# A graph network on 64 graphs: weight preparation in fifteen separately placed steps in place of five, and a second tile for a transposed weight

## Chip, cores and metric

The kernel runs on one core of one Trainium2 chip. The metric is the device time of one execution in microseconds (us), as the median of several runs.

## What is computed

The input is 64 graphs with 256 nodes each, 256 features per node, and a 256x256 adjacency matrix of zeros and ones for each. Two layers are applied. Cut to what matters:

```python
# layer 0: attention with relation masks, 8 heads
q, k = x @ Wq + bq, x @ Wk + bk
attn = softmax(q @ k.T / sqrt(32))
for r in range(4):
    out += (attn * (adj == r)) @ (x @ Wv[r] + bv[r])
x = ln(x + out @ Wo + bo) * g1 + beta1
x = ln(x + gelu(x @ W1 + b1) @ W2 + b2) * g2 + beta2
# layer 1: two graph-attention steps, then a feed-forward
def gat(h, W, a):
    Wh = h @ W
    e = leaky_relu(Wh @ a[:256] + (Wh @ a[256:]).T, 0.2)
    return softmax(where(adj > 0, e, -9e15), axis=1) @ Wh
h = gat(gat(x, L1_W1, a1), L1_W2, a2)
h = ln(x + h) * g_ln1 + b_ln1
y = ln(h + relu(h @ w_ff1 + b_ff1) @ w_ff2 + b_ff2) * g_ln2 + b_ln2
```

All is float32. The feed-forward layers have 1024 hidden features.

## The kernel before

The 64 graphs pass through one after another, as a pipeline: while the second feed-forward of one graph runs, the first of a later graph and the attention of a still later one run too. A graph in the tables of this text counts from 0.

*Stages of a graph.* `load_front` (L185-193) loads the features (`xin`, L190, four DMAs) and the adjacency (`adi`, L192). VectorE transposes the features (`xT`, L529). TensorE makes queries and keys (L558, `qk_ps`), ScalarE copies them out (L567, L569). There are two halves of four heads; for each half TensorE makes four score tiles (L606, `s`), VectorE their row maxima (`nmax`, L611), ScalarE the exponentials (L619, `e`), VectorE the reciprocals (`rden`, L624), ScalarE the normalisation (L629). VectorE transposes 32x32 squares (`eT_sq`, L340), and the rest of the transposition goes through DRAM: a write (L345) and a read (L349) on SyncE's queue (SP). VectorE multiplies by the mask (`pm`, L638), TensorE multiplies with the values (`po`, L653). The values come from `v_ps` (L582) with the weights in seven combinations, as in Strassen's product with seven multiplications. Then follow the output projection (`wo_ps`, L673), a layer norm (L398, the tile `y`), the first feed-forward (`ffa`: up L455, copies L466, adds L472, gelu L478, sums for the seven products on GpSimd L440 and L492, down L503, adds L511), a layer norm, the two graph-attention steps (`ga`, `gb`: L683 to L749, among them `ga_z` at L702, which opens with the copy of a TensorE result on ScalarE), a layer norm, the second feed-forward (`ffb`, with relu) and the last layer norm.

*Buffers.* The score tiles have four PSUM banks with one buffer each, so the second half's scores wait for the first half's exponentials. All other products take one of three PSUM buffers (`mm_tile`).

*Weights and their preparation.* The weights are loaded once by 49 DMAs, all on SP (L864). Some are then prepared once, since biases and gains of the layer norms are folded into the weights that follow:

- `v_weights`: ten VectorE operations that make the value weights' combinations.
- `out_bias` (L289-294): a product on TensorE (`bo_ps`, L292) and an addition.
- `gat_weights` (L296-320): a transposition of the second graph weight (`gw2T`, L303, copy L304), a small product with the attention vectors (`gu`, L311, copy L313), a transposition of the first graph weight (`gw1T`, same lines), and two products (`gext`, L318, copy L320). Both transposes are copied to one tile, `gw[:, 1]`.
- `ffn_weights`, once for each feed-forward (L247-268): 32 matmuls of one column each for the bias (`ffa_b_ps`, `ffb_b_ps`, L253), its addition on VectorE (L255), two activations on ScalarE that apply the gain (L257), four VectorE operations for the up-weights' combinations (L261 to L264), an addition to the row bias (L266), and four VectorE operations for the down-weights' combinations (L275 to L278).

*What sets the order.* The order is written out by hand. A table, `PLACES`, gives each operation of a graph a place; graph g adds g times `PERIOD`. `LOAD_PLACES` gives each weight load a place, and the names `V_PLACE`, `OUT_PLACE`, `GAT_PLACE`, `FFA_PLACE` and `FFB_PLACE` give one to each of the five preparations. Everything is sorted by place and issued in this order, and each engine executes its part in the order of issue. A place is a number for sorting, not a time. A whole preparation is issued at one place, so its instructions stand together on every engine.

Of the kernel before, what the change touches and what calls it, by code (L numbers as in the profile page):

```python
# [9 lines left out]
F32 = mybir.dt.float32  # L10
# [5 lines left out]
ALU = mybir.AluOpType  # L16
AX = mybir.AxisListType

P = 128
# [8 lines left out]
PERIOD = 46.802000  # L28
# [40 lines left out]
    "lg4": 380.3574, "lb4": 381.5864, "store": 394.4577, "te": 551.6675,  # L69
}  # L70
LOAD_PLACES = [
    105.247, 106.338, 251.305, 142.756, 226.120, 202.518, 180.231, 135.528, 193.356, 105.689, 128.568, 205.544,
    225.287, 220.197, 228.322, 220.191, 135.518, 134.198, 236.500, 236.497, 267.691, 145.759, 148.475, 184.117,
    188.115, 118.463, 185.107, 185.099, 138.353, 159.388, 289.336, 256.975, 248.494, 253.344, 263.500, 246.882,
    179.276, 264.537, 240.121, 150.635, 216.481, 224.999, 149.895, 193.794, 257.889, 277.220, 276.101, 310.307,
    239.224,
]
V_PLACE, OUT_PLACE, FFA_PLACE, GAT_PLACE, FFB_PLACE, ODD_PLACE = 135.857, 138.353, 239.224, 193.799, 285.406, 240.000

# [11 lines left out]
def binary_graphs(  # L93
# [13 lines left out]
    nc = tc.nc  # L107
    B, N, D = x.shape
    R = 2
    FF = W1.shape[1]  # L110
    H = 8
    DH = D // H
    KD = D // P
# [3 lines left out]
    EX = D + 4  # L117
    assert (N, D, FF, DH, C, HQ) == (256, 256, 1024, 32, 2, 4)

    const = ctx.enter_context(tc.tile_pool(name="const", bufs=1))  # L120
# [10 lines left out]
    def mm_tile(shape, name, dt=F32):  # L131
        return ps_mm.tile(shape, dt, tag="mm", name=name)
# [5 lines left out]
    ident = const.tile([P, P], F32, name="ident")  # L138
# [14 lines left out]
    def weight(w, name, mixed=False):  # L153

        k, n = w.shape[0] // P, w.shape[1]
        t = const.tile([P, k, n], F32, name=name)
        if mixed:
            mixed_rows(t, w)
        else:
            loads.append((t, w.rearrange("(k p) n -> p k n", p=P)))  # L160
        return t
# [5 lines left out]
    def mixed_vec(v, name):  # L167

        t = const.tile([P, KD, 1], F32, name=name)
        for a in range(A):  # L170
            src = bass.AP(tensor=v.tensor, offset=v.offset + a * S, ap=[[1, S], [P, KD], [1, 1]])
            loads.append((t[a::A], src))
        return t

    def rowvec(v, n, name):
        t = const.tile([P, n], F32, name=name)
        loads.append((t, _row(v, n)))
        return t

    def colvec(v, n, name):  # L180
        t = const.tile([P, n // P], F32, name=name)
        loads.append((t, _col(v, n)))
        return t
# [37 lines left out]
    be1_r, bl1_r = shifts[:, 0], shifts[:, 1]  # L221
    loads.append((be1_r, _row(beta1, D)))
    w1, b1_c = weight(W1, "w1", mixed=True), colvec(b1, FF, "b1_c")
    g1_c, be1_c = mixed_vec(g1, "g1_c"), mixed_vec(beta1, "be1_c")
    w2, b2_r = weight(W2, "w2"), rowvec(b2, D, "b2_r")
    w2_t, f2_t = (const.tile([P, 3, KF // 2, P], F32, name=f"{n}_t") for n in ("w2", "f2"))
    up_t = {n: const.tile([P, 3, FF // 2], F32, name=f"{n}_u") for n in ('ffa', 'ffb')}
    g2_r, be2_r = rowvec(g2, D, "g2_r"), rowvec(beta2, D, "be2_r")
    gw = bp.tile([P, 2, KD, D], F32, tag="ff", name="gw", bufs=3)
    gw1 = gw[:, 0]  # L230
    mixed_rows(gw1, gW1)
    gx = bp.tile([P, KD, EX], F32, tag="wh", name="gx", bufs=2)
    loads.append((gx[:, :, :D], gW2.rearrange("(k p) n -> p k n", p=P)))
    a2c = const.tile([P, KD, 2], F32, name="a2c")
# [4 lines left out]
    gext = const.tile([P, KD, EX], F32, name="gext")  # L239
    gl1_r = rowvec(g_ln1, D, "gl1_r")  # L240
    loads.append((bl1_r, _row(b_ln1, D)))
    f1, bf1_c = weight(w_ff1, "f1", mixed=True), colvec(b_ff1, FF, "bf1_c")
    gl1_c, bl1_c = mixed_vec(g_ln1, "gl1_c"), mixed_vec(b_ln1, "bl1_c")
    f2, bf2_r = weight(w_ff2, "f2"), rowvec(b_ff2, D, "bf2_r")
    gl2_r, bl2_r = rowvec(g_ln2, D, "gl2_r"), rowvec(b_ln2, D, "bl2_r")

    def ffn_weights(w, b, gain, shift, row, shift_row, name, wb, wb_t):  # L247


        p = mm_tile([P, KF], f"{name}_b_ps")  # L250
        for f in range(KF):
            for k in range(KD):
                nc.tensor.matmul(p[:, f:f + 1], w[:, k, f * P:(f + 1) * P], shift[:, k],  # L253
                                 start=(k == 0), stop=(k == KD - 1))
        nc.vector.tensor_tensor(b, p, b, ALU.add)  # L255
        for k in range(KD):
            nc.scalar.activation(w[:, k], w[:, k], AF.Copy, scale=gain[:, k])  # L257
        if name in up_t:
            (a11, a21), (a12, a22) = ([w[:, k, i * FF // 2:(i + 1) * FF // 2] for i in range(2)] for k in range(KD))
            s1, s2, s4 = (up_t[name][:, i] for i in range(3))  # L260
            nc.vector.tensor_tensor(s1, a21, a22, ALU.add)  # L261
            nc.vector.tensor_tensor(s2, s1, a11, ALU.subtract)
            nc.vector.tensor_tensor(s4, a12, s2, ALU.subtract)
            nc.vector.tensor_tensor(a21, a11, a21, ALU.subtract)  # L264
            up_w[name] = {1: a11, 2: a12, 3: s4, 4: a22, 5: s1, 6: s2, 7: a21}
        nc.vector.tensor_tensor(row, row, shift_row, ALU.add)  # L266
        seven[name] = seven_weights([[wb[:, h * KF // 2:(h + 1) * KF // 2, d * P:(d + 1) * P] for d in range(2)]
                                     for h in range(2)], [wb_t[:, i] for i in range(3)])

    seven, up_w = {}, {}  # L270

    def seven_weights(b, t):


        nc.vector.tensor_tensor(t[0], b[0][1], b[1][1], ALU.add)  # L275
        nc.vector.tensor_tensor(t[1], t[0], b[0][0], ALU.subtract)
        nc.vector.tensor_tensor(t[2], b[1][0], t[1], ALU.subtract)
        nc.vector.tensor_tensor(b[0][1], b[0][0], b[0][1], ALU.subtract)  # L278
        return {1: b[0][0], 2: b[1][0], 3: t[2], 4: b[1][1], 5: t[0], 6: t[1], 7: b[0][1]}
# [13 lines left out]
                             start=(k == 0), stop=(k == KD - 1))  # L293
        nc.vector.tensor_tensor(bo_r, p, bo_r, ALU.add)

    def gat_weights():  # L296


        def transposed(w, t, name):
            pt = mm_tile([P, KD, D], f"{name}_ps")  # L300
            for k in range(KD):
                for f in range(KD):
                    nc.tensor.transpose(pt[:, f, k * P:(k + 1) * P], w[:, k, f * P:(f + 1) * P], ident)  # L303
            nc.vector.tensor_copy(t, pt)  # L304
            return t

        w2T = transposed(gx, gw[:, 1], "gw2T")
        pu = mm_tile([P, KD, 2], "gu_ps")
        for k in range(KD):
            for f in range(KD):  # L310
                nc.tensor.matmul(pu[:, k, :], w2T[:, f, k * P:(k + 1) * P], a2c[:, f, :],  # L311
                                 start=(f == 0), stop=(f == KD - 1))
        nc.vector.tensor_copy(gx[:, :, D:D + 2], pu)  # L313
        w1T = transposed(gw1, gw[:, 1], "gw1T")
        for k in range(KD):
            p = mm_tile([P, EX], f"gext_ps{k}")
            for f in range(KD):
                nc.tensor.matmul(p, w1T[:, f, k * P:(k + 1) * P], gx[:, f, :],  # L318
                                 start=(f == 0), stop=(f == KD - 1))
            nc.vector.tensor_copy(gext[:, k, :], p)  # L320

    class Transposed:  # L330

# [181 lines left out]
    class Graph:  # L513
# [166 lines left out]
        def gat_product(self, c):  # L680
            p = self.ps["ga", c] = mm_tile([P, EX], f"ga{self.g}_wps{c}")
            for k in range(KD):
                nc.tensor.matmul(p, self.ht.t[:, c, k, :], gext[:, k, :],  # L683
                                 start=(k == 0), stop=(k == KD - 1))
# [177 lines left out]

    assert len(loads) == len(LOAD_PLACES)
    plan = [(t, len(PLACES), lambda i=i: nc.sync.dma_start(*loads[i])) for i, t in enumerate(LOAD_PLACES)]  # L864
    for place, f in (
            (V_PLACE, v_weights),
            (OUT_PLACE, out_bias),
            ((B - 1) * PERIOD + ODD_PLACE, any_odd),
            (GAT_PLACE, gat_weights),
            (FFA_PLACE, lambda: ffn_weights(w1, b1_c, g1_c, be1_c, b2_r, be1_r, "ffa", w2, w2_t)),  # L870
            (FFB_PLACE, lambda: ffn_weights(f1, bf1_c, gl1_c, bl1_c, bf2_r, bl1_r, "ffb", f2, f2_t))):
        plan.append((place, len(PLACES), f))
    for g in range(B):
        ops = Graph(g).operations()
# [208 lines left out]
@with_exitstack  # L1083
def kernel(ctx: ExitStack, tc: tile.TileContext, *args):
    nc = tc.nc
    pool = ctx.enter_context(tc.tile_pool(name="odd", bufs=1))
    odd = pool.tile([P, 1], I32, name="odd")
    binary_graphs(tc, odd, *args)
    flag = nc.values_load(odd[0:1, 0:1], min_val=0, max_val=1)
    with tc.If(flag > 0):  # L1090
        any_graphs(tc, *args)
# [29 lines left out]
```

## Time and profile before

| what | value |
|---|---|
| median of 3 runs | 3115.67 us (3115.14 to 3116.3) |
| profiled execution | 3118.7 us, its span 3116.9 us |
| TensorE (PE) busy | 3020.8 us (97%), 24797 matmuls |
| VectorE (DVE) busy | 2618.7 us (84%) |
| ScalarE (ACT) busy | 2597.0 us (83%) |
| GpSimd (POOL) busy | 2364.2 us (76%) |
| mean granted TensorE clock | 0.987 |
| data moved by DMA | 457.16 MB, mean 147 GB/s |
| eT write, issue to landing | 3.1 us median |
| eT read, issue to landing | 3.6 us median |

The span is the time from the first to the last event of the profiled execution; 1.8 us of its 3118.7 lie outside it. Busy times are sums over the whole span. In a list of waits, the time is that in which an engine did nothing before the named instruction, and the name behind the arrow is what ended the idle time. The granted clock is the share of full speed at which TensorE was allowed to run; 0.50 is half clock.

### The profile page before, as it was taken

The numbers are of one execution on the slowest core, as the hardware profiler recorded it, in microseconds if no ns is written. First come the engines' busy times: TensorE is split into PE (matmuls) and PEld (weight loads), VectorE is DVE, ScalarE is ACT, GpSimd is POOL, SyncE is SP. The second block draws the span as 40 slices with busy tenths as digits, with TensorE's granted clock in tenths as the row PEclk, the third lists the DMA queues.
The fourth block names the chain that finished last, engine by engine and source line by source line (L and its number), as shares of the span: only waits on it lengthen the run. The fifth ranks groups of instructions, "written<-read, shape, count | busy, mean of one in ns | idle before, by whom it ended". The sixth has DMA issues, their size and how long they took to land.

```text
span 3116.9 us, 72178 instructions
## 1 busy us (share of the span) xinstructions
PE 3020.8 (97%) x24797; PEld 2611.0 (84%) x24797; DVE 2618.7 (84%) x5545; ACT 2597.0 (83%) x7109; POOL 2364.2 (76%) x3142
## 2 busy tenths in 40 slices
PE   6899999999999999999999999999999999999985
PEld 4688888888888888888888888888888888888874
DVE  6888888888888888888888888888888888888852
ACT  5688888888888888888888888888888888888852
POOL 1577777877877877877877877877878777787763
PEclk8899999999999999999999999999999999999997
DMA  7554555455455455455455455455455555445410
GB/s 188 163 158 144 145 162 151 144 160 152 142 157 161 136 160 161 137 157 155 135 160 156 140 156 154 142 154 158 145 147 159 146 146 162 147 143 162 143 50 27
DMA packets 808371, 457.16 MB, mean 147 GB/s; under 512 B 334529, under 2 KB 717377, under 8 KB 808001
## 3 DMA queue, kind: packets, MB, share of 16 engines
q1 hardware_dynamic: 808000, 452.49, 50.3%
q8 instruction: 200, 3.28, 0.5%
q14 instruction: 171, 1.39, 0.1%
HBM read 242.63 MB, written 201.33 MB: 142 GB/s over the span
## 4 chain that ended last, share of the span: by engine, by line
PE 93%; DMA 2%; DVE 2%; ACT 2%; POOL 1%; issue 1%; SPq 0%; POOLq 0%; DVEq 0%; ACTq 0%
PE ffb_ps L455 14%; PE ffa_ps L455 13%; PE ffb_po L503 7%; PE po L653 7%; PE qk_ps L558 7%; PE ffa_po L503 7%; PE v_ps L582 6%; PE ffa_pq L503 6%; PE ffb_pq L503 5%; PE s L606 4%; PE wo_ps L673 4%; PE h_ps L730 4%; PE h_ps L745 3%; PE ga_wps L683 3%; DMA ffa_T<-ffa_T_d 1%
## 5 line engine op out<-in xcount | busy, mean ns | idle before, releaser
L619 ACT ACTIVATE e<-s,nmax 128x256 f32<-128x256 f32 x1024 | 473.6, 476 | 10.6 <-DVE nmax L611 10.4
L629 ACT ACTIVATE e<-e,rden 128x256 f32<-128x256 f32 x1024 | 447.6, 502 | 25.0 <-DVE rden L624 25.0
L638 DVE TENSOR_TENSOR pm<-eT,adT 128x512 f32<-128x512 f32 x512 | 449.5, 899 | 0.0
L340 DVE STREAM_TRANSPOSE eT_sq<-e 128x512 f32<-128x512 f32 x512 | 349.1, 691 | 7.3 <-ACT e L629 6.0
L611 DVE TENSOR_REDUCE nmax<-s 128x2 f32<-128x512 f32 x512 | 341.7, 669 | 2.0 <-PE s L606 2.0
L478 ACT ACTIVATE ffb_h<-ffb_h,bf_c 128x256 f32<-128x256 f32 x512 | 224.9, 503 | 49.0 <-DVE ffb_h L472 49.0
L492 POOL TENSOR_TENSOR ffb_t<-ffb_h 128x512 f32<-128x512 f32 x64 | 81.5, 1273 | 225.8 <-ACT ffb_h L478 225.8
L466 ACT COPY ffb_h<-ffb_ps 128x512 f32<-128x512 f32 x256 | 151.0, 590 | 99.6 <-PE ffb_ps L455 99.5
L472 DVE TENSOR_TENSOR ffb_h<-ffb_ps,ffb_h 128x512 f32<-128x512 f32 x192 | 132.8, 692 | 107.2 <-PE ffb_ps L455 104.2
L466 ACT COPY ffa_h<-ffa_ps 128x512 f32<-128x512 f32 x256 | 148.3, 579 | 83.5 <-PE ffa_ps L455 47.8
L492 POOL TENSOR_TENSOR ffa_t<-ffa_h 128x512 f32<-128x512 f32 x64 | 82.5, 1289 | 172.6 <-PE ffb_pq L503 155.0
L619 ACT ACTIVATION_READ_ACCUMULATOR e<-s,nmax 128x1 f32 x1024 | 211.5, 207 | 0.0
L478 ACT ACTIVATE ffa_h<-ffa_h,b_c 128x256 f32<-128x256 f32 x512 | 211.1, 506 | 0.1
L472 DVE TENSOR_TENSOR ffa_h<-ffa_ps,ffa_h 128x512 f32<-128x512 f32 x192 | 132.3, 689 | 79.7 <-ACT ffa_h L466 45.8
L388 POOL TENSOR_TENSOR rs_x<-rs_x,nhalf 128x2 f32<-128x2 f32 x256 | 182.5, 713 | 21.3
L492 POOL TENSOR_TENSOR ffb_t<-ffb_h,ffb_t 128x512 f32<-128x512 f32 x128 | 163.6, 1278 | 36.3 <-ACT ffb_h L478 35.6
L492 POOL TENSOR_TENSOR ffa_t<-ffa_h,ffa_t 128x512 f32<-128x512 f32 x128 | 185.0, 1445 | 5.0
L591 DVE TENSOR_TENSOR v<-v,v_ps 128x256 f32<-128x256 f32 x448 | 177.2, 407 | 2.0 <-PE v_ps L582 1.1
L398 ACT ACTIVATE ffa_res<-ffa_res,nb_x,rs_x 128x256 f32<-128x256 f32 x256 | 139.9, 595 | 25.2 <-POOL nb_x L393 24.8
L455 PE MATMUL ffb_ps<-ffb_T,f 128*128 128x128 f32 x1024 | 130.7, 283 | 26.7 <-DMA ffb_T<-ffb_T_d 22.9
L606 PE MATMUL s<-kT,qT 32*128 32x256 f32 x2048 | 149.8, 407 | 7.0 <-ACT e L619 6.0
L558 PE MATMUL qk_ps<-xT,wq 128*128 128x256 f32 x512 | 141.1, 399 | 15.9 <-DVE xT L529 8.4
(192 smaller groups left out, 9799.1 us busy)
## 6 DMA issues: line engine op xcount, KB each, us to landing
eT_d<-eT_sq SPq DMA_DIRECT2D x512, 256.0 KB, 3.1
eT<-eT_d SPq DMA_DIRECT2D x512, 256.0 KB, 3.6
xin<-in_x_dram SPq DMA_DIRECT2D x256, 64.0 KB, 3.6
adi<-in_adj_dram SPq DMA_DIRECT2D x64, 256.0 KB, 2.6
y<-in_x_dram SPq DMA_DIRECT2D x64, 256.0 KB, 2.9
ffa_T_d<-ffa_T_sq SPq DMA_DIRECT2D x64, 256.0 KB, 2.8
ffa_T<-ffa_T_d SPq DMA_DIRECT2D x64, 256.0 KB, 2.9
hT_d<-hT_sq SPq DMA_DIRECT2D x64, 256.0 KB, 2.1
```

Source lines behind the costliest of these rows:

```text
L340: nc.vector.transpose(self.sq.rearrange("p a c k y -> p (c k) a y"), src.rearrange("p c (k a x) -> p (c k) a x", k=KD, a=A))
L455: nc.tensor.matmul(self.ps[bank][:, f], w[:, f * P:(f + 1) * P], b, start=(i in (1, 2, 5) and f == 0), stop=(f == KF // 2 - 1), skip_group ...
L466: nc.scalar.copy(self.half_of(*{1: (0, 0), 6: (0, 1), 7: (1, 1), 4: (1, 0)}[i]), self.ps[0])
L478: nc.scalar.activation(h, h, self.func, bias=self.ba[:, f0 + f:f0 + f + 1])
L492: nc.gpsimd.tensor_tensor(out, a, b, ALU.subtract)
L503: nc.tensor.matmul(self.p[bank][:, k], a[:, f], seven[self.name[:3]][i][:, f], start=(f == 0), stop=(f == KF // 2 - 1))
L558: nc.tensor.matmul(p[:, i, :], w[:, k, m * P:(m + 1) * P], self.xT[:, k, :], start=(k == 0), stop=(k == KD - 1))
L606: nc.tensor.matmul(self.s4[m][h][:, ic * N:(ic + 1) * N], self.qT[hp, m, ic * P:(ic + 1) * P], self.kT[hp, m, :], start=True, stop=True)
L611: nc.vector.tensor_reduce(self.nmax[m, h], self.s4[m][h].rearrange("p (c n) -> p c n", c=C), AX.X, ALU.max, negate=True)
L619: nc.scalar.activation(e[:, ic, :], self.s4[m][h][:, ic * N:(ic + 1) * N], AF.Exp, bias=self.nmax[m, h][:, ic:ic + 1], accum_out=self.den[ ...
L629: nc.scalar.activation(e[:, ic, :], e[:, ic, :], AF.Copy, scale=self.rden[m, h][:, ic:ic + 1])
L638: nc.vector.tensor_tensor(self.pm[m, h].rearrange("p c k (b y) -> p (c k) b y", b=A), t.rearrange("p b c k y -> p (c k) b y"), self.adT.re ...
```

## The change

The five preparations become fifteen steps, each with a place of its own in a list `PREPARE`: `v_weights`, `out_bias`, then bias, gain, up-weights and down-weights of the first feed-forward, the transposition of the second graph weight, the small product, the transposition of the first graph weight, the two products, and the four steps of the second feed-forward. The copy of the first graph weight's transpose goes to a new tile, `gwT`, which takes 2 KB in each partition. All 49 loads get new places. The table of the graphs' own operations and the period are unchanged.

```diff
-V_PLACE, OUT_PLACE, FFA_PLACE, GAT_PLACE, FFB_PLACE, ODD_PLACE = 135.857, 138.353, 239.224, 193.799, 285.406, 240.000
+PREPARE = [168.9447, 186.6319, 201.8244, 232.9996, 235.5957, 255.9105, 192.6586, 194.5093, 211.4569, 221.6303, 240.2005, 283.2526, 312.9662, 314.7084, 279.8160]
+ODD_PLACE = 240.000
...
-    def ffn_weights(w, b, gain, shift, row, shift_row, name, wb, wb_t):
+    def ffn_bias(w, b, shift, name):
...
+    def ffn_gain(w, gain):
...
+    def ffn_up(w, name):
...
+    def ffn_down(row, shift_row, name, wb, wb_t):
...
+    gwT = const.tile([P, KD, D], F32, name="gwT")
...
+    def gat_transposed(w, t, name):
...
+    def gat_right():
...
+    def gat_product(k):
+        p = mm_tile([P, EX], f"gext_ps{k}")
+        for f in range(KD):
+            nc.tensor.matmul(p, gwT[:, f, k * P:(k + 1) * P], gx[:, f, :], start=(f == 0), stop=(f == KD - 1))
+        nc.vector.tensor_copy(gext[:, k, :], p)
...
+    steps = [v_weights, out_bias,
+             lambda: ffn_bias(w1, b1_c, be1_c, "ffa"), lambda: ffn_gain(w1, g1_c), lambda: ffn_up(w1, "ffa"),
+             lambda: ffn_down(b2_r, be1_r, "ffa", w2, w2_t),
+             lambda: gat_transposed(gx, gw[:, 1], "gw2T"), lambda: gat_right(),
+             lambda: gat_transposed(gw1, gwT, "gw1T"), lambda: gat_product(0), lambda: gat_product(1),
+             lambda: ffn_bias(f1, bf1_c, bl1_c, "ffb"), lambda: ffn_gain(f1, gl1_c), lambda: ffn_up(f1, "ffb"),
+             lambda: ffn_down(bf2_r, bl1_r, "ffb", f2, f2_t)]
+    for place, f in [*zip(PREPARE, steps), ((B - 1) * PERIOD + ODD_PLACE, any_odd)]:
```

In the sorted order this gives the following moves, by the neighbours on each engine:

| step | engine | stood before | stands after the change |
|---|---|---|---|
| v_weights | VectorE | ahead of a row maximum of graph 0, first half | behind the first eT_sq of graph 0, ahead of xT of graph 1 |
| out_bias | TensorE | ahead of scores 1 of graph 0 | in graph 1's values, between v_ps 2 and 5 |
| gw2T, gu | TensorE | ahead of scores 1 of graph 1 | the same |
| ffa bias | TensorE | behind the values v3 of graph 1, ahead of scores 1 of graph 2 | behind v_ps 4, ahead of po 0 of graph 0 |
| its addition | VectorE | behind v3 | ahead of a row maximum of graph 1, second half |
| gw1T | TensorE | behind gu | behind the ffa bias |
| gext, two products | TensorE | behind gw1T | ahead of qk 0, and ahead of scores 1, of graph 2 |
| ffa gain | ScalarE | behind the exponentials 0-3 of graph 2 | behind the key copy of graph 2, ahead of the norm of y of graph 0 |
| ffa up-weights | VectorE | behind the bias addition | behind the ffa transposition of graph 0, ahead of a row maximum of graph 2 |
| ffa down-weights | VectorE | behind the up-weights | among the adds of graph 0's ffa |
| ffb bias | TensorE | behind graph 3's first values | the same |
| ffb gain | ScalarE | ahead of the exponentials 0-0 of graph 3 | behind the exponentials 1-1 of graph 3 |
| ffb up-weights | VectorE | behind the bias addition | about 30 us later, ahead of a reciprocal of graph 3's second half |
| ffb down-weights | VectorE | behind the up-weights | ahead of a row maximum of graph 3, first half |
| loads on SP | SyncE | 15 ahead of the second graph's xin, w2 among them | 17, without w2 |

The number of instructions on each engine is the same in both kernels.

## The prediction

> **What bounds the kernel now.** I first read busy time, waits and the granted clock by stretches of the span (columns: stretch, length, then busy time and instructions of PE, PEld, DVE, ACT, POOL, granted clock, DMA share, GB/s).
>
> ```profile
> 20.00:40.00 20.00, 11.71 (x64) 8.48 (x64) 14.03 (x31) 15.84 (x54) 1.06 (x2) 0.74 0.69 177
> 40.00:60.00 20.00, 13.78 (x86) 8.80 (x90) 13.47 (x31) 8.21 (x30) 4.04 (x7) 0.83 0.66 176
> ...
> 100.00:120.00 20.00, 19.61 (x129) 15.77 (x130) 13.53 (x36) 14.13 (x40) 7.37 (x13) 0.87 0.65 183
> 120.00:140.00 20.00, 13.97 (x84) 11.77 (x83) 18.12 (x29) 8.97 (x22) 9.17 (x8) 0.79 0.41 111
> ...
> 300.00:1000.00 700.00, 700.00 (x5818) 607.54 (x5819) 611.45 (x1299) 610.13 (x1675) 557.28 (x745) 1.00 0.52 152
> ```
>
> From about 150 us on TensorE is never idle (700.00 of 700 us), at full clock. It is the bound there, and one graph costs one fixed period of its work. The order of instructions with their waits, compared for both programs on every engine, is the same from about 165 us on; no matmul, no vector operation and no byte is added or removed. So whatever the change does, it does while the first four graphs fill the pipeline: by 160 us TensorE has been idle for 40.25 us, and a delay of TensorE there passes to the end one for one. Where the 40 us lie, the waits of TensorE from 0 to 160 us tell (total, times, longest):
>
> ```profile
> PE qk_ps L558 <- DVE xT L529: 8.4, 2, 5.8
> ...
> PE s L606 <- ACT e L619: 6.0, 2, 3.1
> PE ffa_ps L455 <- ACT ga_z L702: 5.6, 1, 5.6
> PE gu_ps L311 <- DVE gw L304: 2.9, 1, 2.9
> ```
>
> Another 7.6 us is the wait for the first weight. The last two belong to weight preparation: the gw copy (L304) reaches VectorE behind attention work, and ga_z comes late through a chain which the timeline shows (start, length, engine, line; the bracket is idle time before it):
>
> ```profile
> 69.09 3.63 PE L253 MATMUL ffa_b_ps<-be_c,w 128*128 128x1 f32 x32
> ...
> 75.67 2.09 PE L606 MATMUL s<-kT,qT 32*128 32x256 f32 x16 [2.96 <-ACT e L619]
> ...
> 112.45 4.75 PE L253 MATMUL ffb_b_ps<-bl_c,f 128*128 128x1 f32 x32
> ...
> 117.25 0.17 DVE L255 TENSOR_TENSOR bf_c<-ffb_b_ps,bf_c 128x8 f32<-128x8 f32 x1 [1.50 <-PE ffb_b_ps L253]
> ...
> 125.95 1.21 DVE L278 TENSOR_TENSOR f<-f 128x512 f32<-128x512 f32 x1
> ...
> 127.92 0.91 ACT L629 ACTIVATE e<-e,rden 128x256 f32<-128x256 f32 x2 [6.62 <-DVE rden L624]
> ...
> 129.60 2.08 PE L455 MATMUL ffa_ps<-ffa_T,w 128*128 128x128 f32 x8 [5.57 <-ACT ga_z L702]
> 131.47 3.90 PE L455 MATMUL ffa_ps<-ffa_xt,ffa_u 128*128 128x128 f32 x16
> ```
>
> From 117.25 to 127.16 VectorE does nothing but prepare the second feed-forward weights (nine operations, 8.28 us of work and 1.63 us waiting for the gain on ScalarE). rden stands behind them, ScalarE waits 6.62 us for it, ga_z comes after, TensorE loses 5.57 us and then runs at half clock: 16 matmuls in 3.90 us, against 1.79 at full clock.
>
> **The change, step by step.** The sum is made against the profiled execution, 3118.7 us (span 3116.9 and 1.8 around it), which is 3.0 above the median of 3115.67; I add the difference to the median. I follow how late TensorE is at named points.
>
> *Loads and v_weights, to 30 us.* 17 in place of 15 loads of about 0.6 us stand on SP ahead of the second graph's xin, which adds 1.2 us. But w2 (1 MB) is no longer among them: the issue at 20.67 us came free when w2 landed (7.86 us after its issue), so xin moves from 22.01 to about 20.9. That gains nothing: v_weights, ten operations, 9.17 to 14.52 us before, beside TensorE's first qk and scores, now stand just ahead of xT of graph 1 on VectorE, behind the first eT_sq. Replayed with their own durations xT ends at 29.6 to 30.3 in place of 28.40. TensorE at qk of graph 1 (28.53): **+1.9**. out_bias leaves the front, where its add waited 2.16 us; ScalarE was late there anyway (scores at 20.91 waited for e), so 0.3 at most, taken as nothing.
>
> *Graph-attention weights in five steps, to 47 us.* The out-bias matmuls (0.86) come in ahead of gw2T. gu still waits for the copy of gw2T, at 41.38+1.9+0.9 = 44.2. But gw1T, its copy and the two gext products (42.43 to 47.48, 5.05 us, 3.83 of it gext at half clock against 1.75 for eight equal matmuls at full clock) leave this place. Scores 1 of graph 1 (47.48): +2.8-5.05 = **-2.3**. gext goes to places beside qk of graph 2 and scores of graph 2; each half is 0.9 us of TensorE warm, paid as work in both programs. The tile of its own takes away the wait of the second copy for gu's reads, and 2 KB per partition; no instruction reads it more slowly by anything in the profile, so nothing, on either side.
>
> *First bias product ahead of graph 0's masked products, to 58 us.* ffa_b (32 matmuls) moves from 69.09 to about here. It needs the fourth piece of w1, whose load now follows eT writes of graph 0 on SP: issue about 45.0, landing 4.5 us later at the least (w1's pieces took 4.5 to 7.2) gives 49.5. TensorE is at it by 48.1 and waits 1.4 us. Its duration is 3.63 at full clock; half clock is not shown for all of it, but the second one ran half its way so in 4.75, so 2x3.6 = 7.2 bounds it. The Trainium skill ("TensorE: Matmul & The Clock Gate", HAM oscillation) puts the limit at gaps over about 3.4 us; the gap ahead of gu is 2.9, so by the rule the clock stays up and ffa_b costs 3.6. This trace has half clock (0.50, 43.5 to 49 us) behind just such a gap of 2.85, and again behind 2.96 at 75.67; and in ffb_b it falls to 0.54 with no gap at all. I take the row: mostly cold, about 5.4. The bias add now stands on VectorE ahead of nmax of scores 1 (50.74 before), so VectorE has to wait from about 48.6 for it: to 53.3 warm, 56.9 cold. Behind it are nmax, the gw1T copy (0.65), then xT of graph 2. qk of graph 2 (57.52): **+5** (3.2 to 6.8). Queued behind the add are also that graph's exponentials, through nmax.
>
> *Gain and up-weights ahead of scores, to 76 us.* The two gain activations (2.19) move ahead of the y normalisation; they stood in this same chain before (72.53, ahead of the last e), so they cancel. But ffa_up, four operations of 0.69 after the feed-forward transpose, now stands ahead of nmax of graph 2; before, it ran beside scores 1. The chain from kT (68.50) to scores 1 (75.67) grows from 7.1 to 9.8: +2.6, **+7.6** in all. From there ffa_T has landed and the 1.11 us at 82.66 go; ffa_down (4 us of VectorE) is in part ahead of what the third product waits for, +0.3. At 100 us: **+6.8** (4.6 to 9).
>
> *Second feed-forward in four, to 136 us.* ffb_down (0.67+0.94+0.83+1.63+1.21 = 5.28) runs ahead of nmax of graph 3, in large part while TensorE has the bias product (4.75); ffb_up (2.8) goes to about 153; the gain goes behind the second softmax half, so VectorE no longer waits 1.63 for it. rden comes at about 120.2 in place of 127.9 on the old scale, so TensorE's 5.57 shrink to about 1.1: -4.5. If the clock then stays up, 2.08+3.90 become 3.6: -2.4; half clock from the bias product itself is not removed, so I count half, -1.2. nmax and va behind ffb_down: +0.6. Sum -5.1 (bounds -3 and -8). At 136 us: **+1.7**.
>
> *Gain and ffb_up at 150 us.* 2.19 on ScalarE, of which 1.42 fall into idle time, and 2.8 on VectorE ahead of a reciprocal: kT's copy and the output projection behind it are late by 0 to 2.3, taken 1.2: **+2.9** at 160 us. From there everything is the same.
>
> So 3115.7+2.9 = 3118.6 us (3121.6 for a profiled run like the one shown). The likeliest case's own range: -2 to +6.2, 3113.7 to 3121.9.
>
> **Rivals.** *A: the clusters are all that costs.* If w1 lands by 48.1 and ffa_b runs warm, the add is done at 51.9 and qk of graph 2 is only 1.8 late; if half of ffa_up falls beside waits, scores 1 are 3.1 late, +2.0 at 100 us; the 5.57 and the half clock behind it go whole, -8, and the eight ga_wps matmuls, 3.81 at half clock now, run warm at 1.75, about -1 after idle time. -7.0, **3108.7**. For it: VectorE's 9.9 us block is the largest single avoidable stall. Against: loads queued behind transposes have landed late throughout (16 engines 0.93 busy from 46 to 49 us).
> *B: slower.* One mechanism: VectorE, in order, stands behind the bias product at about 50 us and then behind ffa_up. It decides from an add that ends after about 56 us: +6.8 at qk of graph 2, +9 at 100 us. If the second block, too, gives back only 3 us, since the half clock comes from the bias product, and the gain at 150 costs 2.3: +8.3, **3124.0**. For it: four half-clock stretches follow such stalls in the trace. Against: ScalarE's long waits (7.20 at 48.12, 6.62 at 127.92) leave slack that takes up some.
> *C: it doesn't do what it says.* The work is spread but each idle microsecond is only moved, and the fill is bound by xin, e and the layers' own latency (waits for xT and e make 14.4 of the 40.25): 0, **3115.7**. That lies within the likeliest case's range.
>
> **How the numbers follow.** 0.2% is 6.2 us, about what a measurement can tell from no change: 3109.4 to 3121.9. The likeliest case with C has 0.47, A 0.25 and B 0.28; A and B are given the two sides. Range: A's time with a little of what lies below, B's with 2 us above, 3107.5 to 3126; about 0.1 is left out on each side.
>
> **What would show it.** Right: TensorE at qk of graph 1 near 30.4; scores 1 of graph 1 near 45; VectorE idle some 4 to 8 us ahead of the bias add at about 53 to 56; scores 1 of graph 2 near 83; the wait for ga_z under 2 us; a period of 46.3 us from 160 us on, shifted by what the fill lost. Wrong: a bias add without a wait before it (A), a half clock from 50 to 58 us with ffa_b over 6 us (B), or any new gap on TensorE after 165 us, which would break the argument that only the fill counts.

## The result, and the profile after

The changed kernel is slower: the median of seven runs is 3129.76 us (3124.01 to 3130.62), against 3116.3 us for the kernel before in seven runs next to them (3114.19 to 3123.42). The ratio is 1.0029, with a 95% interval of 1.0016 to 1.0042, or 5 to 13 us. Single executions of one kernel lie up to 7 us from its median here, so a part of the change is judged below by its stretch of the trace first, and by the ratio second. Each ratio below compares with executions of the kernel before from the same batch; the medians of that kernel lie between 3116.3 and 3121.2 us in the four batches, so only ratios can be compared from batch to batch. The profiled execution took 3124.75 us, with a span of 3123.0; it is 6.1 longer than the span before.

First the stretches, with the same columns as before:

```profile
20.00:40.00 20.00, 12.77 (x59) 8.86 (x53) 14.55 (x35) 12.97 (x43) 1.07 (x2) 0.62 0.68 192
40.00:60.00 20.00, 16.31 (x104) 12.46 (x103) 11.32 (x26) 4.78 (x15) 3.93 (x6) 0.66 0.58 162
60.00:80.00 20.00, 12.92 (x90) 8.87 (x88) 14.57 (x34) 15.62 (x48) 3.64 (x7) 0.99 0.74 221
...
120.00:140.00 20.00, 17.08 (x107) 13.79 (x107) 14.98 (x31) 11.78 (x34) 6.34 (x8) 0.83 0.71 185
...
300.00:1000.00 700.00, 698.69 (x5827) 604.75 (x5825) 610.51 (x1298) 610.00 (x1671) 555.84 (x744) 1.00 0.52 150
```

From 120 to 140 us TensorE is busy longer than before (17.08 in place of 13.97), from 60 to 80 less (12.92 in place of 16.59). From 40 to 60 it is busier (16.31 in place of 13.78), with 104 matmuls in place of 86, since the first bias product with its 32 now stands here, and at a clock of 0.66 in place of 0.83. After the fill the two kernels are nearly alike again (1.3 us of idle time in 700, before none). The waits of TensorE up to 175 us (total, times, longest):

```profile
PE s L599 <- ACT e L612: 11.5, 2, 7.8
...
PE v_ps L575 <- DVE wv L288: 5.2, 1, 5.2
PE ffa_pq L496 <- DVE w_t L281: 3.3, 1, 3.3
PE gu_ps L313 <- DVE gw L307: 2.7, 1, 2.7
PE wo_ps L666 <- ACT kT L562: 2.5, 2, 2.2
...
PE qk_ps L551 <- DVE xT L522: 1.2, 1, 1.2
```

The wait of 5.57 us for ga_z is gone. New are 7.8 us ahead of scores 1 of graph 2, 3.3 for the down-weights and 2.2 ahead of the output projection. The timeline shows where each comes from:

```profile
28.47 0.70 DVE L522 STREAM_TRANSPOSE xT<-xin 128x512 f32<-128x512 f32 x1
...
47.50 6.96 PE L252 MATMUL ffa_b_ps<-be_c,w 128*128 128x1 f32 x32 [0.99 <-PE v_ps L575]
54.50 0.17 DVE L254 TENSOR_TENSOR b_c<-ffa_b_ps,b_c 128x8 f32<-128x8 f32 x1 [7.53 <-PE ffa_b_ps L252]
...
82.41 2.09 PE L599 MATMUL s<-kT,qT 32*128 32x256 f32 x16 [7.82 <-ACT e L612]
...
95.40 1.64 DVE L280 TENSOR_TENSOR w_t<-w_t,w 128x512 f32<-128x512 f32 x1
96.45 1.72 POOL L485 TENSOR_TENSOR ffa_t<-ffa_h 128x512 f32<-128x512 f32 x1
97.08 1.64 DVE L281 TENSOR_TENSOR w_t<-w,w_t 128x512 f32<-128x512 f32 x1
98.87 1.13 PE L496 MATMUL ffa_pq<-w_t,ffa_h 128*128 128x128 f32 x8 [3.30 <-DVE w_t L281]
...
120.26 3.63 PE L252 MATMUL ffb_b_ps<-bl_c,f 128*128 128x1 f32 x32
...
161.73 3.62 PE L666 MATMUL wo_ps<-wo,oT 128*128 128x256 f32 x8 [2.17 <-ACT kT L562]
```

VectorE stands still for 7.53 us ahead of the addition of the first bias, since the product before it ran wholly at half clock: 6.96 us in place of 3.63. The row of TensorE for this stretch (length, busy time, granted clock, DMA share, GB/s) shows it:

```profile
46.00:58.00 12.00, 11.01 (x63) 0.50 0.60 166
```

The 0.99 us ahead of the product, put down to `v_ps` by the profile, are more likely the wait for the last piece of w1: it was issued at 44.3 and landed 3.1 us later, at 47.4. Two of the down-weight operations take 1.64 us while GpSimd works beside them, and TensorE waits for the second of them.

The next table cuts the fill at the starts of the score products: s(g,h) is half h of graph g. Each number is the microseconds from one start to the next in the profiled execution. It keeps a loss in its place, whatever happened ahead of it. Each row is a single execution.

| kernel | to s(1,0) | to s(1,1) | to s(2,0) | to s(2,1) | to s(3,0) | to s(3,1) | to s(4,0) |
|---|---|---|---|---|---|---|---|
| before | 33.39 | 14.09 | 16.96 | 11.23 | 32.14 | 13.00 | 39.02 |
| changed | 34.71 | 9.63 | 24.55 | 13.52 | 33.19 | 13.00 | 37.11 |
| difference | +1.3 | -4.5 | +7.6 | +2.3 | +1.1 | 0 | -1.9 |
| tile only (from before) | 34.87 | 13.72 | 18.05 | 11.25 | 32.13 | 13.50 | 38.63 |
| first bias late (from changed) | 37.81 | 9.34 | 18.94 | 17.13 | 34.89 | 12.99 | 35.51 |
| ffb early (from changed) | 35.63 | 9.34 | 24.63 | 13.51 | 32.96 | 12.99 | 36.08 |
| up-weights behind maxima (from changed) | 37.45 | 9.35 | 24.37 | 10.85 | 35.50 | 12.99 | 36.89 |
| the same, down-weights in a gap | 35.10 | 9.56 | 24.25 | 11.45 | 31.66 | 12.68 | 34.60 |
| ffa together (from changed) | 34.95 | 9.59 | 19.07 | 11.68 | 34.14 | 13.01 | 35.04 |
| ffb split only (from before) | 33.30 | 13.85 | 18.12 | 11.24 | 32.15 | 13.38 | 34.15 |
| graph weights only (from before) | 32.72 | 8.98 | 19.87 | 11.40 | 36.70 | 13.23 | 37.65 |
| ffb split, early (from before) | 33.13 | 14.10 | 16.90 | 11.24 | 32.27 | 13.50 | 33.62 |
| wide bias products (from before) | 32.27 | 13.74 | 18.07 | 11.29 | 32.14 | 13.20 | 37.44 |
| wide bias and ffb early (from before) | 33.84 | 15.48 | 16.76 | 11.28 | 32.86 | 12.96 | 33.83 |
| value weights first (from changed) | 32.90 | 9.48 | 25.20 | 13.50 | 34.69 | 13.00 | 36.77 |

The differences add up to +5.9 us at s(4,0), and the span grew by 6.1. In the first column chance is large: the six kernels with the changed front part (the changed one and the five made from it that keep v_weights late) have a mean of 35.9, the seven with the old front part 33.4. The front costs some 2.6 us, not 1.3. In the other columns, too, kernels with the same order differ, by up to 1.8 us (the second column of the kernels that keep the graph weights in one block: 13.72 to 15.48).

That the stretches give the whole difference is in part luck. From s(4,0) to the end of the span it takes 2957.1 us before and 2957.3 after, but in the fourteen profiled executions of this text between 2956.5 (tile only) and 2966.2 (first bias late). TensorE still waits there now and then, in the kernel before 2.55 us between 1000 and 2000 us, and its last graphs drain the pipeline with waits and half clock. So what a kernel gains in the fill can be hidden at the end of a single execution.

### The profile page after: what moved, and what is told of

Its sections match the earlier page's. It is cut to its first block, busy times and chain, and to the rows that moved or that the text cites. A ratio compares the mean times of both kernels' runs of the same rounds, so it can differ in the third digit from the quotient of the medians.

```text
span 3123.0 us, 72174 instructions
## 1 busy us (share of the span) xinstructions
PE 3021.9 (97%) x24797; PEld 2610.0 (84%) x24797; DVE 2619.8 (84%) x5545; ACT 2601.0 (83%) x7109; POOL 2366.1 (76%) x3142
## 4 chain that ended last, share of the span: by engine, by line
PE 91%; DVE 3%; ACT 2%; DMA 1%; POOL 1%; issue 1%; SPq 0%; POOLq 0%; DVEq 0%; ACTq 0%
PE ffb_ps L448 14%; PE ffa_ps L448 13%; PE ffb_po L496 7%; PE qk_ps L551 7%; PE po L646 7%; PE ffa_po L496 7%; PE v_ps L575 6%; PE ffa_pq L496 5%; PE ffb_pq L496 5%; PE s L599 4%; PE wo_ps L666 4%; PE h_ps L723 3%; PE ga_wps L676 3%; PE h_ps L738 3%; DMA ffa_T<-ffa_T_d 1%
## 5 line engine op out<-in xcount | busy, mean ns | idle before, releaser
L448 PEld LDWEIGHTS ffb_ps<-ffb_T,f 128*128 128x128 f32 x1024 | 127.2, 196 | 32.4 <-issue 20.3
```

The source lines that it names most:

```text
L448: nc.tensor.matmul(self.ps[bank][:, f], w[:, f * P:(f + 1) * P], b, start=(i in (1, 2, 5) and f == 0), stop=(f == KF // 2 - 1), skip_group ...
```

## The experiments

Theory 1 was that the positions of the steps make the loss, each in its own stretch, and that most of it is kept to the end. The rivals were the tile, the slack of the fill, and the clock.

**The tile alone.** The five preparations in their old order, in the new code, with the old places of the loads, so that only `gwT` is left of the change:

```diff
-PREPARE = [168.9447, 186.6319, 201.8244, 232.9996, 235.5957, 255.9105, 192.6586, 194.5093, 211.4569, 221.6303, 240.2005, 283.2526, 312.9662, 314.7084, 279.8160]
+PREPARE = [135.857, 138.353, 239.224, 239.224, 239.224, 239.224, 193.799, 193.799, 193.799, 193.799, 193.799, 285.406, 285.406, 285.406, 285.406]
```

> The order of the kernel before, with the second transposed graph weight in the new tile as the only difference. Theory 1 (the positions make the loss): nothing, within 1 us of the kernel before. Rival (the 2 KB tile or the lifted wait for gu's reads matters): half a microsecond to 1 us faster at the gext products, or anything slower.

Ratio to the kernel before 0.9999 (0.9991 to 1.0008). The stretches are those of before within the scatter. The tile has no effect that can be seen (the interval is 2.8 us less to 2.5 more); what remains of the change is the places of the steps and of the loads.

In the edits that follow, short names stand for entries of `PREPARE`: `v` for the value weights, `abias`, `again`, `aup`, `adown` for the four steps of the first feed-forward, `bgain`, `bup`, `bdown` for those of the second, `gw1T`, `gx0`, `gx1` for the last three of the graph weights. "On the kernel before" means the kernel of the last run, with the old places.

**The first bias product late.** In the changed kernel:

```diff
-    abias = 201.8244
+    abias = 232.9
```

> The changed kernel with the first bias product and its addition put back to just ahead of the gain, behind graph 1's values. Theory 1 (VectorE stands behind the bias product at half clock, each microsecond lost in the fill is kept): qk of graph 2 comes at about 55 in place of 61.96, of which 3.6 are paid again at the new place; 3 to 4 us faster than the changed kernel. Rival (the fill has slack behind it, so a lost microsecond at 50 us is given back by 80): scores 1 of graph 2 stay near 82, within 1 us of the changed kernel.

The stretch to s(2,0) fell by 5.6 us, and those behind it grew by 3.6 and 1.7: ratio to before 1.0031 (1.0020 to 1.0042), nothing won over the changed kernel. The rival's number came true (scores 1 of graph 2 at 83.22, within 1 us of 82.41), though part of the gain is hidden in it, since the front of this execution was 3.1 us later. The rival's reason does not hold. What happens is in the timeline of this run:

```profile
69.42 4.62 PE L246 MATMUL ffa_b_ps<-be_c,w 128*128 128x1 f32 x32
73.65 2.19 ACT L252 ACTIVATE w<-w,g_c 128x1024 f32<-128x1024 f32 x2 [3.46 <-PE ffa_b_ps L246]
...
83.22 2.09 PE L593 MATMUL s<-kT,qT 32*128 32x256 f32 x16 [5.53 <-ACT e L606]
```

The gain scales the weights that the bias product reads, so it waits for the product (3.46 us), and the norm of y, the feed-forward transposition and the exponentials stand behind the gain on ScalarE. As long as the gain stands ahead of that chain, the bias product is paid for early or late. It is not slack that gives the time back; it is the same chain, entered at another point.

**Gain and up-weights of the second feed-forward earlier.** In the changed kernel:

```diff
-    bgain, bup = 312.9662, 314.7084
+    bgain, bup = 288.0, 293.0
```

> The changed kernel with the gain and the up-weights of the second feed-forward moved ahead, the gain behind the last exponentials of graph 3's first half, the up-weights into the 3.7 us in which VectorE waits for ga_z. Theory 1: the wait of 2.17 us ahead of the output projection at 161.7 and the half clock behind it (3.62 in place of 2.05) go, 3.7 us faster than the changed kernel. Rival (they only move to the ga_z chain): less than 1 us.

The wait ahead of the output projection and the half clock behind it went (wo_ps 2.06 us in place of 3.62). But a wait of 1.03 us for a value addition, at 135.74 in the changed kernel, became 2.85: VectorE makes the up-weights ahead of it. The last stretch is 1.0 shorter, not 3.7. Ratio to before 1.0026 (1.0015 to 1.0036). The rival was nearer: what is won at one wait is mostly lost at another.

**Up-weights of the first feed-forward behind the row maxima.** In the changed kernel:

```diff
-    aup = 235.5957
+    aup = 239.4
```

> The changed kernel with the four up-weight operations of the first feed-forward behind the row maxima of graph 2 in place of ahead of them. Theory 1: scores 1 of graph 2 come 2.0 to 2.7 us earlier than 82.41 and the end with them, 2 us faster than the changed kernel. Rival (the gain on ScalarE, which stands in the same chain, is what holds it): under 0.7 us.

The stretch to s(2,1) fell by 2.67 us, the four operations' own 2.7: theory 1's place and size. The next stretch gave 2.3 back: the down-weights still came late (a wait of 3.31 us), and the first sixteen up products ran longer at half clock, 3.62 in place of 2.48. Ratio to before 1.0018 (1.0010 to 1.0026); the part kept at the end is 3 us by the ratios, 0.4 by the two stretches, so its size is not settled, and the two ratios' intervals overlap.

**Down-weights in a gap, too.** On top of the last edit:

```diff
-    adown = 255.9105; load of w2 at 233.593
+    adown = 234.4;    load of w2 at 218.0
```

> The changed kernel with the first feed-forward's up-weights behind the row maxima (as in the run that moves them alone) and its down-weights, with the load of w2 ahead of them, in the 2.6 us in which VectorE waits for the norm of y. Theory 1 (in the changed kernel the down-weights fall beside GpSimd's sums, where three of their operations take 1.64 to 1.75 us in place of 0.69, and TensorE waits 3.3 us for them and then runs at half clock): the wait ahead of the first down product goes, from scores 1 of graph 2 to its last down product 23.0 to 24.5 us in place of 25.6 (27.9 with the up-weights moved alone), 3 to 4 us faster than the changed kernel. Rival (the third product is bound by gelu or by GpSimd anyway): a wait of the same length with another name, under 1 us.

The wait ahead of the down product is gone, and from scores 1 of graph 2 (80.36) to the last down product of graph 0 (104.42) it takes 24.1 us, in place of 27.9 with the up-weights moved alone. Ratio to before 1.0014 (1.0007 to 1.0020): 4.7 us of the changed kernel's 9 are won back by both moves together (by the two intervals, some 0.2 to 9; an estimate). Its timeline shows the same two operations without GpSimd beside them, and the first down products without the wait for them:

```profile
74.72 0.69 DVE L274 TENSOR_TENSOR w_t<-w_t,w 128x512 f32<-128x512 f32 x1
75.44 0.69 DVE L275 TENSOR_TENSOR w_t<-w,w_t 128x512 f32<-128x512 f32 x1
...
94.57 0.71 PE L490 MATMUL ffa_pq<-w_t,ffa_h 128*128 128x128 f32 x4
```

In the changed kernel GpSimd worked from 94.92 to 102.9 us without a break of more than 0.1. So these two operations took 0.95 us more each at the place that the change gave them.

**The first feed-forward together again.** In the changed kernel, its four steps next to each other at the old place:

```diff
-    abias, again, aup, adown = 201.8244, 232.9996, 235.5957, 255.9105
+    abias, again, aup, adown = 239.15, 239.16, 239.17, 239.18
```

> The changed kernel with the four steps of the first feed-forward back together at their old place behind graph 1's values; loads, graph weights and second feed-forward as changed. Theory 1 (the split of the first feed-forward makes the loss, the other splits gain): from scores 1 of graph 1 to scores 1 of graph 2 29 us in place of 38.1, and the whole 7 to 9 us faster than the changed kernel, 2 to 3 us faster than the one before. Rival (the loads' new order makes the loss): the stretch stays above 34.

From s(1,1) to s(2,1) it takes 30.75 us in place of 38.07: 7.3 of the loss come from the split of the first feed-forward. The ratio to before is 1.0011 (1.0002 to 1.0020), 5.6 us better than the changed kernel (by the two intervals, some 0.7 to 10.5; an estimate). The rival, the new order of the loads, forecast more than 34 for the stretch and fails. It is not faster than the kernel before, as theory 1 had it; the front part, which this run keeps, and the graph weights, whose gain comes to nothing in a run below, were missing in that sum.

**The second feed-forward's split alone**, on the kernel before:

```diff
-    bgain, bup, bdown = 285.406, 285.406, 285.406
+    bgain, bup, bdown = 312.9662, 314.7084, 279.816
```

> The kernel before, with only the second feed-forward's gain, up-weights and down-weights at their new places (and the second tile). Theory 1: the wait of 5.4 us for ga_z goes, and 3.7 us come back at the output projection near 160 us; from scores 0 of graph 3 to scores 0 of graph 4 50.0 in place of 52.0, 2 us faster than the kernel before. Rival (as predicted: 3.9 us faster), or nothing.

From s(3,0) to s(4,0) 47.5 us in place of 52.0: 4.5 us shorter. The wait for ga_z is gone, and the 2.17 ahead of the output projection is there, but at full clock (wo_ps 1.99). Six other kernels have this wait of 2.17 us; the product took 1.99 to 2.00 us in three of them and 3.54 to 3.64 in the other three. Here:

```profile
153.83 1.99 PE L660 MATMUL wo_ps<-wo,oT 128*128 128x256 f32 x8 [2.17 <-ACT kT L556]
```

The stretch is nearer to the rival's size, the prediction's own. Ratio 0.9994 (0.9985 to 1.0002): at the end the gain is not clear of noise.

**The graph weights' split alone**, on the kernel before:

```diff
-    gw1T, gx0, gx1 = 193.799, 193.799, 193.799
+    gw1T, gx0, gx1 = 211.4569, 221.6303, 240.2005
```

> The kernel before, with only the transposition of the first graph weight and the two products at their new places (and the second tile). Theory 1: scores 1 of graph 1 come 4.4 us earlier after scores 0 (9.3 to 9.7 in place of 14.1); TensorE's later waits for xT take back part, 1 to 3 us faster than the kernel before at the end. Rival (all is taken back at xT of graph 2, which is bound by VectorE and xin): from scores 0 of graph 1 to qk of graph 2 still 24 us, no difference at the end.

The stretch to s(1,1) fell from 14.1 to 9.0, and the next ones took it back: +2.9, +0.2 and +4.6. Ratio 1.0002 (0.9993 to 1.0010). The rival is right that no gain is left, but its place is not: from scores 0 of graph 1 to qk of graph 2 it takes 21.9 us, not 24, against 24.1 before. Of the +2.9 some 2.1 are the moved work itself (gw1T 1.06 and the first gext product 1.04 us now lie there). The +4.6 begin at ffa_T of graph 0, which comes no earlier, while the scores do:

```profile
78.31 2.04 PE L442 MATMUL ffa_ps<-ffa_T,w 128*128 128x128 f32 x8 [2.10 <-DMA ffa_T<-ffa_T_d]
80.89 2.08 PE L442 MATMUL ffa_ps<-ffa_T,w 128*128 128x128 f32 x8 [0.54 <-DVE gext L315]
82.76 3.62 PE L442 MATMUL ffa_ps<-ffa_xt,ffa_u 128*128 128x128 f32 x16
```

The wait takes 2.1 us. From 70 to 85 us the granted clock is 0.50 in this run, and the sixteen matmuls at 82.76 take 3.62 us, where the kernel before has 2.09 at 82.66; there the clock was back by 81 us.

**The second feed-forward's split alone, early**, on the kernel before:

```diff
-    bgain, bup, bdown = 285.406, 285.406, 285.406
+    bgain, bup, bdown = 288.0, 293.0, 279.816
```

> The kernel before with only the second feed-forward split (and the second tile), its gain and up-weights at the earlier places of the run that moved them alone: gain behind the last exponentials of graph 3's first half, up-weights where VectorE waits for ga_z. Theory (the split of the second feed-forward is the part of the change that gains, and the wait at the output projection is its price): no wait of 2.2 us at 153.8, from scores 0 of graph 3 to scores 0 of graph 4 46 to 47.5 us (52.0 before, 47.5 with the change's places), 4 us or more faster than the kernel before. Rival (the up-weights only push the values' additions back, as a wait of 2.85 us showed when they were moved in the changed kernel): 47.5 or more, no gain on the change's places.

47.1 us from s(3,0) to s(4,0), ratio 0.9994 (0.9986 to 1.0003): the same as with the change's own places. The wait at the output projection went, and one of 2.37 us for a value addition came. The stretch lies in the theory's range, 0.4 below that of the change's own places, which is within the scatter, and 4 us at the end are not shown. So no difference between these two places of VectorE's 2.8 us is shown; what both have in common is that they are not in one block with the rest.

**Wide bias products**, on the kernel before:

```diff
-        p = mm_tile([P, KF], f"{name}_b_ps")
+        p = mm_tile([P, KF, 64], f"{name}_b_ps")
...
-                nc.tensor.matmul(p[:, f:f + 1], w[:, k, f * P:(f + 1) * P], shift[:, k],
+                nc.tensor.matmul(p[:, f], w[:, k, f * P:(f + 1) * P], shift[:, k].to_broadcast([P, 64]),
...
-        nc.vector.tensor_tensor(b, p, b, ALU.add)
+        nc.vector.tensor_tensor(b, p[:, :, 0], b, ALU.add)
```

> The kernel before (with the second tile), with the two bias products made 64 columns wide (each matmul's moving column repeated 64 times, the first of the 64 results used); the order is the same. Theory A (the half clock behind the bias products comes from these products, whose array is almost idle between weight loads of one column's work): the granted clock stays at 1.00 through and behind both products, ga_wps takes 1.75 in place of 3.8 us, and the stretch from scores 0 to scores 1 of graph 3 loses 1 to 2.5 of its 13.0 us. Theory B (the half clock comes from the waits of TensorE around them): half clock as before, the products 3.6 to 4.8, no difference.

The second product took 3.68 us, at full clock, where four kernels with the narrow one and the same order ahead of it took 4.75 to 5.22. In these four the clock fell within the product; with 64 columns it did not, here and in the next run, which speaks for theory A as to the product itself. At full clock the narrow product is no slower (3.63). And the half clock came all the same, now behind a wait of 1.28 us, and ga_wps took 3.66, where 1.92 is its time at full clock. For the time, theory B's forecast of no difference holds. The timeline:

```profile
112.16 3.68 PE L246 MATMUL ffb_b_ps<-bl_c,f 128*128 128x64 f32 x32
117.12 3.66 PE L670 MATMUL ga_wps<-gext,hT 128*128 128x260 f32 x8 [1.28 <-DMA hT<-hT_d]
```

and the stretches of TensorE (busy time, granted clock, DMA):

```profile
114.00:116.00 2.00, 1.84 (x17) 1.00 0.99 182
116.00:118.00 2.00, 0.88 (x3) 0.82 0.93 252
118.00:120.00 2.00, 2.00 (x6) 0.50 0.52 131
```

The stretch from s(3,0) to s(3,1) stays at 13.2: what the product saves, TensorE waits for hT. Ratio 0.9996 (0.9988 to 1.0005).

**Both**, on the kernel before: wide bias products with the early places of the second feed-forward.

```diff
-    bgain, bup, bdown = 285.406, 285.406, 285.406
+    bgain, bup, bdown = 288.0, 293.0, 279.816
...
-                nc.tensor.matmul(p[:, f:f + 1], w[:, k, f * P:(f + 1) * P], shift[:, k],
+                nc.tensor.matmul(p[:, f], w[:, k, f * P:(f + 1) * P], shift[:, k].to_broadcast([P, 64]),
```

> The kernel before with both: wide bias products, and the second feed-forward split with early gain and up-weights. If both effects are real they add up, 5 to 7 us faster than the kernel before; if they gain the same wait, 4.

Ratio 0.9993 (0.9985 to 1.0002), 46.8 us from s(3,0) to s(4,0). The effects do not add up. Three kernels with the second feed-forward split on the old order lie at 0.9993 to 0.9994, and each interval includes 1: perhaps 2 us faster, not shown.

**Value weights first**, in the changed kernel:

```diff
-    v = 168.9447
+    v = 135.857
```

> The changed kernel with the value weights back at their old place, ahead of the first row maxima of graph 0; nothing else. Theory 1 (at the new place they stand ahead of xT of graph 1 on VectorE and cost 2 us there): the waits of 5.2 and 2.0 us for wv and VectorE ahead of qk of graph 1 become one of 4 to 5, qk of graph 1 near 27.5 in place of 29.3 (29.7 to 32.5 in the other runs of this order), about 2 us faster than the changed kernel. Rival (xin comes too late either way): qk not earlier than 29.

xT comes as soon as VectorE's transposes ahead of it are done, and qk of graph 1 at 27.75:

```profile
26.94 0.67 DVE L516 STREAM_TRANSPOSE xT<-xin 128x512 f32<-128x512 f32 x1
27.75 2.05 PE L545 MATMUL qk_ps<-xT,wq 128*128 128x256 f32 x4 [4.56 <-DVE xT L516]
```

The six kernels with late value weights have qk of graph 1 at 29.3 to 32.5, mean 30.6. Ratio to before 1.0019 (1.0009 to 1.0029), about 3 us better than the changed kernel, with overlapping intervals. Theory 1 holds at this place; that the gain is kept to the end is not shown. The new places of the loads were not tried by themselves.

## Why the prediction was right or wrong

The direction was right, and so were the named places and the path through VectorE; the size was too small: 2.9 us forecast, 9 measured (5 to 13), or 6.1 in the one profiled execution. By the ratio the time is 3124.7 us, inside the range; the plain median, 3129.76, lies above it. The likeliest case, no difference beyond 0.2%, is not what the ratio's middle shows (its interval begins at 0.16%); rival B's 3124.0 is nearer in size, and the sign set for B appeared, half clock from 50 to 58 us and a first bias product over 6 us. B's other step did not: it let the second feed-forward's block give back only 3 us. Step by step:

- *Only the fill counts.* Right for this pair: the sum of the stretches up to s(4,0) is +5.9, the span's difference +6.1. That TensorE is never idle from 150 us on is too strong. After the change it waits for ffa_T's transfer for 1.3 us between 300 and 1000, the new gap that was named as a sign of being wrong; but the kernel with the second feed-forward split early has 1.0 there and the one with the first together none, and before, 2.55 us come between 1000 and 2000. These waits differ from profile to profile also where the order of before is kept, so nothing shows that they are the change's, and they blur a sum of the fill by some us.
- *Loads and v_weights, +1.9 at qk of graph 1.* Right in cause: taking v_weights back brings qk to 27.75. In the profiled execution it is +0.8 (29.32), over all kernels +2.4.
- *Graph weights, scores 1 at -2.3.* It was at 44.34, -3.1. Right in place and size. That all of it is taken back later was not foreseen in this form: the run of this part alone ends with no gain. The sum carried the gain on as if it were kept, and the losses behind it came out as if they were all new.
- *First bias product, qk of graph 2 at +5.* It was at 61.96, +4.4. In part luck: the start was put at 49.5 and came at 47.50, the duration was set at 5.4 us between 3.6 and 7.2 and was 6.96, all of it at half clock. The two errors nearly cancel (end forecast 54.9, measured 54.46). The row of the trace was the right guide here, against the rule that the prediction takes from the Trainium skill ("TensorE: Matmul & The Clock Gate", HAM oscillation), a gap of about 3.4 us: half clock came some 2 us after a gap of 2.69 had ended.
- *Gain and up-weights, scores 1 of graph 2 at +7.6.* It was at 82.41, +6.7. The stretch grew by 2.3 where 2.6 were forecast, and moving the up-weights alone took 2.67 off it.
- *Down-weights, +0.3.* This term was mis-sized: the wait is 3.30 us, and the products behind it ran partly at half clock (ffa_pq 1.13, then ffa_po 1.58 and 3.10 where 1.16 and 2.05 are usual). I had counted their 4 us of VectorE beside other work and had not looked at who works on GpSimd at that moment. The Trainium skill ("GPSIMD Engine Reference", 1. Specifications) says that GpSimd shares its SBUF interface with VectorE operations that have two SBUF inputs; these are such, and here they take 1.64 us beside GpSimd's sums and 0.69 without them. That the shared interface is the reason rests on that page; the runs show the two durations and the moments.
- *Second feed-forward, -5.1.* From 108.00, where the last down product of graph 0 was +7.8, to the h_ps product at 138.13, +2.0: -5.8. Right; alone on the kernel before, this split shortens its stretch by 4.5, where the prediction's two terms give -3.9.
- *Gain and up-weights at 150 us, +1.2 (0 to 2.3).* Mis-sized: +3.9. The wait is 2.17, at the upper end, and the output projection behind it ran at half clock, 3.62 in place of 2.07, which the bound had not taken in. In three of the seven kernels with this wait of 2.17 us half clock came (3.54 to 3.64), in four it did not (1.99 to 2.00, the run with the split alone among them), so this second part is not fixed by the order of the work.

So the terms that failed are the two smallest of the sum. For the down-weights the wait itself was mis-sized, 3.30 us where 0.3 were allowed; for the second gain the wait was within its bounds, and the half clock behind it was left out. Between the 6.1 us of the profiled execution and the 9 of the ratio, 1.3 may be the front part, which is 2.6 over all kernels; the rest is not assigned.

Why the change loses, then: one split, that of the first feed-forward, costs 7.3 us of the fill, the new front, with v_weights as its shown part, some 2.6, and the splits that help, graph weights and second feed-forward, are worth 4.5 and some 2 us where they stand; of the first no gain is seen at the end, and of the second about 2 us, not clear of noise. What stays open is the share of each at the end of the run, since single executions of a kernel differ by more than these parts.

## What to carry to other kernels

Splitting a block of preparation into steps helped here only as far as the steps held up nothing at their new places; ask of every step what stands behind it in the queue, above all where steps depend on each other (bias, gain, weights) and drag each other ahead of the main chain. A time won ahead of a transfer that is no earlier is not won; follow it to the next wait that it doesn't move. And when a wait of TensorE is added, count the products behind it at half clock as one of the cases: behind the same wait of 2.17 us three kernels of seven had it.

## What was not expected of the hardware

Behind the second bias product ga_wps ran at half clock in all fourteen profiled executions (3.53 to 3.84 us for eight matmuls, where 1.92 is the time at full clock in the same view), with waits from none to 1.28 us between the two. With 64 columns it was the same. So a wait is not needed for it, and the wider product did not prevent it.

The first bias product, 32 matmuls with one column each, took 6.96 us in all five kernels that have it at the changed place; in the changed kernel the clock was 0.50 from 46 to 58 us and was down when the product began. In the kernel before, half clock lasted from about 43 to 50, 74 to 80.5 and 115 to 121.5 us (estimates from the granted clock of stretches of 0.5 to 1 us), each time about half as long. The second bias product took 4.75 to 5.22 us in four kernels, in which the clock fell within it with no wait ahead of it, and 3.68 with 64 columns; in the other eight kernels narrow ones took 3.63 to 3.79. What the clock reacts to, these runs don't settle; they show that it can fall while TensorE counts as busy without a break, in a product of one column.
